# The spectral filter's channel product in two halves of 64 stationary columns

## The chip, the cores and the metric

The kernel runs on one core of a Trainium2 chip. A core has a matrix engine (TensorE, PE in the profile; its weight loads are listed apart as PEld), three engines for elementwise work (VectorE, DVE; ScalarE, ACT; GpSimd, POOL) and SyncE (SP), which here issues the DMAs. The metric is the device time of one launch in microseconds (us); the median of several runs counts.

## The reference

Four layers over an image batch of 4 x 64 x 64 x 96 (4096 tokens, 96 channels an image): a selective-scan block, a separable convolution, linear attention with a quantized feed-forward part, and a spectral filter with another such part. Only one step of the spectral filter is concerned:

```python
h = jnp.einsum('bnc,hc->bnh', x, w1)                      # 96 -> 192 channels
h = jax.nn.relu(_bn(h, ...))
X = jnp.fft.fft(h, axis=1, norm='ortho')                  # over the 4096 tokens
xr = jax.nn.relu(X.real * rd - X.imag * idg + rb)
xi = jax.nn.relu(X.imag * rd + X.real * idg + ib)
y = jnp.fft.ifft(xr + 1j * xi, axis=1, norm='ortho').real
o = jnp.einsum('bnh,ch->bnc', y, w2)                      # 192 -> 96 channels
return _bn(o, ...)
```

The last product is over channels alone and the inverse transform over tokens alone, so the kernel makes the product ahead of the inverse transform: on the real and on the imaginary part of every frequency.

## The kernel before

All arithmetic of this step is in float32. The 4096-point transform is made in two stages of 64 points each. For each image `filter_in` makes the first channel product (p_h), the gate, and the first stage (p_dft, L1337), and stores the result in DRAM (`z_s`). `filter_mid` is the stage that the change touches. It takes the 64 values of one index four at a time (`k0` = 0, 4, ..., 60: 16 groups an image). For one group it loads a piece `zl` of `z_s` (384 KB, L1362) and a piece `tw` of the table of the second stage (256 KB, L1366), each with three buffers and issued two groups ahead. Then TensorE makes

- p_dft2a (L1394): 8 products, stationary 128 x 64, moving 128 x 128, whose outputs go in turn to partitions 0 to 63 and 64 to 127 of a bank of PSUM. After the eviction `ya` holds 128 channels of four indices, with 64 frequencies of real and 64 of imaginary part side by side.
- p_dft2b (L1403): 4 products of the same kind, for the other 64 channels of the four indices, evicted into `yb`.
- p_o (L1377 and L1378): the channel product of the group before. For each of four indices `j` two products are summed in PSUM: `ya[:, j, :]` (128 channels x 128 frequencies) is stationary and the weights `w2a` (128 x 96) move; then `yb` with `w2b`, whose other half of rows is zero. The result has 128 frequency rows and 96 channels, and its eviction `os<-p_o` (L877 or L881) goes into `os_`.

After the 16 groups `filter_turn` (p_idft, L1443) and `filter_out` (p_idft, L1482) make the inverse transform.

TensorE takes a float32 product as two passes, each with a weight load and a matmul in the trace: the 64 x 4 products of L1377 stand there as 512.

Where the stage runs differs by image. Images 0 to 2 do it beside the scans of later image halves. The scans are the main work: for chunks of 128 x 1024 VectorE runs two scans and an addition (L1908, L1959, L1969), GpSimd two multiplications (L1645, L1649), ScalarE the decay `pa` (L1662) that each scan needs, and TensorE sums over states in `reduce` (py, L1676), into groups of 32 PSUM partitions. The order on each engine there is the program's: `pieces` is called after every scan step and lets the generators of the side work go on as far as their credit by engine reaches; a `yield (2.4, 0, 0, 0)` in `filter_mid` asks for 2.4 units of TensorE before a group of p_o. In that part all evictions of the stage are ScalarE's (`evacuate`), in the same queue as the decays. Image 3 is done in the tail, with no scans left; there evictions go to ScalarE and VectorE in turn, and eight banks of PSUM serve the stage in place of three.

`reduce` has an order that is of use below: where a chunk was kept apart (`dl`), it adds two terms into the same 32 partitions and then goes to the next 32:

```python
for j in (2 * c + k for c in chunks for k in range(2)):
    terms = [Ss[n, q]] + ([dls[n, 0]] if q == 0 and n in apart else [])
    for i, x in enumerate(terms):
        nc.tensor.matmul(py[32 * j : 32 * j + 32, :], lhsT=red, rhs=x[...], ...)
```

Of the kernel before, what the change touches and what calls it, by code (L numbers as in the profile page):

```python
# [30 lines left out]
N1 = 64  # L31
# [42 lines left out]
def layers(ctx: ExitStack, tc: tile.TileContext, a: dict, out):  # L74
# [4 lines left out]
    nc = tc.nc  # L79
# [43 lines left out]
    def steps_past(since, n):  # L123

        while ordered[0] and clock[0] < since + n:
            yield NEXT
# [746 lines left out]
    def evacuate(dst, src, relu=False):  # L873

        flip[0] ^= 1
        if ordered[0] or flip[0]:
            nc.scalar.activation(dst, src, AF.Relu if relu else AF.Copy)  # L877
        elif relu:
            nc.vector.tensor_scalar(dst, src, 0.0, None, ALU.max)
        else:  # L880
            nc.vector.tensor_copy(dst, src)  # L881
# [13 lines left out]
    def rest(b, take, deep, x1t=None, held=None):  # L895
# [461 lines left out]
        def filter_mid(wk, os_):  # L1357


            def load(k0):  # L1360
                z = wk.tile([128, 3, 4, N1], F32, tag="zl", name="zl", bufs=3)
                nc.sync.dma_start(  # L1362
                    z.rearrange("p h k c -> p h (k c)"), z_s[b][:, :, k0 * N1 : (k0 + 4) * N1]
                )
                tw = wk.tile([128, 4, 128], F32, tag="tw", name="tw", bufs=3)
                nc.sync.dma_start(tw, a["dft2"][:, k0 : k0 + 4, :])  # L1366
                return z, tw, clock[0]

            nxt = [load(0), load(4)]
            yield (0, 0, 0, 0, 5)  # L1370
            yield NEXT
            yield NEXT
            before = None

            def project(k0, ya, yb, po):
                for j in range(4):
                    nc.tensor.matmul(po[:, j, :], lhsT=ya[:, j, :], rhs=w2a, start=True, stop=False)  # L1377
                    nc.tensor.matmul(  # L1378
                        po[:, j, :], lhsT=yb[:, j // 2, :], rhs=w2b[:, j % 2, :],
                        start=False, stop=True,  # L1380
                    )

            for k0 in range(0, N1 + 4, 4):
                if k0 < N1:
                    pa, give_a = yield from take("p_dft2a", 128)
                    pa = pa.rearrange("p (k m) -> p k m", m=128)
                    z, tw, since = nxt.pop(0)
                    yield from steps_past(since, LANDING)
                    yield (2.4, 0, 0, 0, 2.6)
                    if k0 + 8 < N1:  # L1390
                        nxt.append(load(k0 + 8))
                    for j in range(4):
                        for hc in range(2):
                            nc.tensor.matmul(  # L1394
                                pa[hc * N1 : (hc + 1) * N1, j, :], lhsT=z[:, hc, j, :],
                                rhs=tw[:, j, :], start=True, stop=True,
                            )
                    pb, give_b = yield from take("p_dft2b", 128, 256)
                    pb = pb.rearrange("p (k m) -> p k m", m=128)
                    yield (0.8, 0.6, 0, 0)  # L1400
                    for j in range(4):
                        at = N1 * (j % 2)
                        nc.tensor.matmul(  # L1403
                            pb[at : at + N1, j // 2, :], lhsT=z[:, 2, j, :], rhs=tw[:, j, :],
                            start=True, stop=True,
                        )
                    ya = wk.tile([128, 4, 128], F32, tag="ya", name="ya", bufs=2 * deep)
                    evacuate(ya, pa, relu=True)
                    give_a()
                if before is not None:  # L1410
                    po, give = yield from take("p_o", 128, 4 * C)
                    po = po.rearrange("p (k c) -> p k c", c=C)
                    yield (2.4, 0, 0, 0)
                    project(*before, po)
                if k0 < N1:
                    yield (0, 0.4, 0, 0)
                    yb = wk.tile([128, 2, 128], F32, tag="yb", name="yb", bufs=2 * deep)
                    evacuate(yb, pb, relu=True)
                    give_b()
                if before is not None:  # L1420
                    yield (0, 0.5, 0, 0)
                    evacuate(
                        os_[:, :, before[0] : before[0] + 4], po.rearrange("p k c -> p c k")
                    )
                    give()
                before = (k0, ya, yb)
# [384 lines left out]
    aside, weights, head, start = Region(tc), Region(tc), Region(tc), Region(tc)  # L1811
# [300 lines left out]
```

## Time and profile before

| | |
|---|---|
| median of 3 runs | 5775.93 us (5759.04 to 5779.57) |
| the profiled execution, its own time | 5793.85 us |
| its span, first to last instruction | 5792.0 us |
| busy, share of the span: TensorE, VectorE, ScalarE, GpSimd | 72%, 84%, 52%, 76% |
| TensorE's mean granted clock | 0.764 of full |
| p_o: passes recorded (L1377 and L1378) | 512 and 512, median 275 ns each |
| p_dft2a: passes recorded | 1024, median 273 ns |
| ScalarE's waits for p_o (`os<-p_o`) | 79.5 us, 42 times |

A line of the timeline or of the chain has the start in microseconds from the start of the span, the duration, engine, line, operation, and the tiles written and read; "x2" after it is the number of instructions merged in it, and the bracket at the end is how long the engine stood idle before it and what released it. The time of a matmul in the trace holds its way through the array: passes that follow each other overlap, so the distance between their starts is what one costs.

### The profile page before, as it was taken

The numbers are of one execution on the slowest core, as the hardware profiler recorded it, in microseconds if no ns is written. First come the engines' busy times: TensorE is split into PE (matmuls) and PEld (weight loads), VectorE is DVE, ScalarE is ACT, GpSimd is POOL, SyncE is SP. The second block draws the span as 40 slices with busy tenths as digits, with TensorE's granted clock in tenths as the row PEclk, the third lists the DMA queues.
The fourth block names the chain that finished last, engine by engine and source line by source line (L and its number), as shares of the span: only waits on it lengthen the run. The fifth ranks groups of instructions, "written<-read, shape, count | busy, mean of one in ns | idle before, by whom it ended". The sixth has DMA issues, their size and how long they took to land. (4 is left out here: it accounts for less than half of the span.)

```text
span 5792.0 us, 65076 instructions
## 1 busy us (share of the span) xinstructions
PE 4191.9 (72%) x19770; PEld 1625.2 (28%) x19770; DVE 4882.4 (84%) x3649; ACT 3015.3 (52%) x4184; POOL 4418.5 (76%) x2164
## 2 busy tenths in 40 slices
PE   8878887879855776664576776666777667667778
PEld 4422222222211221241331221334222124323346
DVE  4188988888899898998799999999999999878564
ACT  4767766766663356545444446435544544434233
POOL 1488887888898788888778989888898898867200
PEclk9889897888866876666677876668778666877788
DMA  4388868876799878788988868679987678986013
GB/s 123 113 216 227 237 195 240 230 212 189 203 255 234 225 206 227 208 236 244 250 232 229 220 184 221 197 216 249 233 229 202 169 207 235 254 224 177 23 42 102
DMA packets 470107, 1174.80 MB, mean 203 GB/s; under 512 B 90768, under 2 KB 155900, under 8 KB 469628
## 3 DMA queue, kind: packets, MB, share of 16 engines
q1 hardware_dynamic: 469756, 1170.64, 74.1%
q8 instruction: 157, 2.57, 0.2%
q14 instruction: 194, 1.59, 0.1%
HBM read 1013.53 MB, written 156.76 MB: 202 GB/s over the span
## 5 line engine op out<-in xcount | busy, mean ns | idle before, releaser
L1649 POOL TENSOR_TENSOR S<-S,rep 128x1024 f32<-128x1024 f32 x768 | 1807.6, 2356 | 560.7 <-DVE S L1969 518.2
L1662 ACT ACTIVATE pa<-dl,nega 128x1024 f32<-128x1024 f32 x1152 | 1285.0, 1117 | 1446.7 <-DVE S L1969 1086.7
L1645 POOL TENSOR_TENSOR B<-B,rep 128x1024 f32<-128x1024 f32 x768 | 1798.6, 2357 | 114.3 <-DMA B<-du_s 54.2
L1908 DVE TENSOR_TENSOR_SCAN S<-pa,S,B 128x1024 f32<-128x1024 f32 x576 | 1352.8, 2349 | 316.1 <-ACT pa L1662 130.1
L1676 PE MATMUL py<-S,red 128*32 128x512 f32 x3072 | 916.3, 853 | 753.0 <-POOL S L1649 509.6
L1959 DVE TENSOR_TENSOR_SCAN pa<-pa,edge,B 128x1024 f32<-128x1024 f32 x438 | 1029.7, 2351 | 50.7 <-ACT pa L1662 50.7
L1969 DVE TENSOR_TENSOR S<-S,pa 128x1024 f32<-128x1024 f32 x630 | 763.6, 1212 | 1.9
L1908 DVE TENSOR_TENSOR_SCAN S<-pa,B 128x1024 f32<-128x1024 f32 x192 | 436.6, 2274 | 50.2 <-ACT pa L1662 36.3
L1676 PEld LDWEIGHTS py<-S,red 128*32 128x32 f32 x3072 | 110.4, 126 | 1238.0 <-POOL S L1649 708.9
L1959 DVE TENSOR_TENSOR_SCAN pa<-pa,B 128x1024 f32<-128x1024 f32 x192 | 441.0, 2297 | 5.3
L402 PE MATMUL p_conv<-low,conv_w 128*96 128x512 f32 x864 | 437.6, 658 | 10.1 <-ACT u L414 7.6
L154 ACT COPY side<-side 96x256 f32<-96x256 f32 (+1 forms) x448 | 279.2, 630 | 176.2 <-DMA deltaT_s<-side 74.9
L1959 DVE TENSOR_TENSOR_SCAN dl<-pa,edge,B 128x1024 f32<-128x1024 f32 x138 | 323.1, 2341 | 21.0 <-ACT pa L1662 9.3
L1250 POOL CAST h<-y 128x1536 fp8e5<-128x1536 f16 x64 | 95.5, 1492 | 305.2 <-ACT y L886 284.1
L1654 POOL TENSOR_TENSOR dl<-dl,rep 128x1024 f32<-128x1024 f32 x138 | 325.7, 2360 | 0.1
L402 PE MATMUL p_conv<-high,conv_w 64*96 64x512 f32 (+1 forms) x576 | 266.3, 599 | 0.0
L1072 PE MATMUL p_mean<-t,centre 96*96 96x512 f32 x256 | 176.4, 801 | 100.8 <-ACT sq L1064 48.1
L1676 PE MATMUL py<-dl,red 128*32 128x512 f32 x552 | 227.9, 742 | 24.2 <-POOL dl L1654 24.2
L402 PEld LDWEIGHTS p_conv<-low,conv_w 128*96 128x96 f32 x864 | 149.4, 181 | 315.6 <-issue 289.2
L1684 ACT COPY ys<-py 128x512 f32<-128x512 f32 x384 | 221.9, 578 | 20.0 <-PE py L1676 16.3
L647 PE MATMUL p_y<-side,ident 96*96 96x512 f32 x336 | 208.2, 767 | 33.4 <-DVE q L1115 11.0
L953 PE MATMUL p_l<-x,taps 96*96 96x504 f32 (+3 forms) x432 | 206.2, 630 | 16.0 <-DMA x<-x 12.1
(262 smaller groups left out, 6035.1 us busy)
## 6 DMA issues: line engine op xcount, KB each, us to landing
dl<-delta_s SPq DMA_DIRECT2D x768, 256.0 KB
B<-du_s SPq DMA_DIRECT2D x768, 256.0 KB
B<-duT_s SPq DMA_DIRECT2D x768, 256.0 KB
dl<-deltaT_s SPq DMA_DIRECT2D x768, 256.0 KB
z_s<-z SPq DMA_DIRECT2D x48, 512.0 KB
zl<-z_s SPq DMA_DIRECT2D x64, 384.0 KB
side<-y_s SPq DMA_DIRECT2D x120, 192.0 KB
rep<-bc_s SPq DMA_DIRECT2D x64, 256.0 KB
```

Source lines behind the costliest of these rows:

```text
L154: nc.scalar.copy(o.rearrange("p (w h) -> p w h", h=HW), t[:n, :].rearrange("p (h w) -> p w h", w=HW)[:, q * w : (q + 1) * w, :],)
L402: nc.tensor.matmul(p, lhsT=conv_w[: src.shape[0], k, oc * C : (oc + 1) * C], rhs=src[:, ky : ky + RPB, kx : kx + HW], start=(k == 0), stop ...
L647: nc.tensor.matmul(p, lhsT=ident[:C, :C], rhs=x, start=(j == 0), stop=(j == 2))
L1645: nc.gpsimd.tensor_tensor(Bs[n, q], Bs[n, q], reps[n // NG, 0, q], ALU.mult)
L1649: nc.gpsimd.tensor_tensor(Ss[n, q], Ss[n, q], reps[n // NG, 1, q], ALU.mult)
L1654: nc.gpsimd.tensor_tensor(dls[n, 0], dls[n, 0], reps[n // NG, 1, 0], ALU.mult)
L1662: nc.scalar.activation(pa, dls[n, q], AF.Exp, scale=nega[:, g : g + 1])
L1676: nc.tensor.matmul(py[32 * j : 32 * j + 32, :], lhsT=red, rhs=x[:, k * BLK : (k + 1) * BLK], start=(i == 0), stop=(i == len(terms) - 1),)
L1684: nc.scalar.copy(ys, pys.pop((n, half)))
L1908: nc.vector.tensor_tensor_scan(s, pas[q], Bs[n, q], Ss[n, q - 1][:, CH - 1 : CH] if q else 0.0, ALU.mult, ALU.add,)
L1959: nc.vector.tensor_tensor_scan(to[:, ::-1], pas[q][:, ::-1], Bs[n, q][:, ::-1], edge if k else 0.0, ALU.mult, ALU.add,)
L1969: nc.vector.tensor_tensor(Ss[n, q], Ss[n, q], to, ALU.add)
```

## The change

For each index `j` the two products of p_o are made twice, with 64 of the 128 stationary columns each: first frequencies 0 to 63 into partitions 0 to 63 (`ya` part, then `yb` part), then 64 to 127 into partitions 64 to 127. What is computed is the same, and so are the tiles, their buffers and the evictions.

```diff
             def project(k0, ya, yb, po):
                 for j in range(4):
-                    nc.tensor.matmul(po[:, j, :], lhsT=ya[:, j, :], rhs=w2a, start=True, stop=False)
-                    nc.tensor.matmul(
-                        po[:, j, :], lhsT=yb[:, j // 2, :], rhs=w2b[:, j % 2, :],
-                        start=False, stop=True,
-                    )
+
+                    for at in (slice(0, N1), slice(N1, 128)):
+                        nc.tensor.matmul(
+                            po[at, j, :], lhsT=ya[:, j, at], rhs=w2a, start=True, stop=False
+                        )
+                        nc.tensor.matmul(
+                            po[at, j, :], lhsT=yb[:, j // 2, at], rhs=w2b[:, j % 2, :],
+                            start=False, stop=True,
+                        )
```

`N1` is 64.

## The prediction

> **What bounds the kernel now.** I read the slices first, then the chain that ended last, then timelines of the places where p_o stands.
>
> ```profile
> PE   8878887879855776664576776666777667667778
> DVE  4188988888899898998799999999999999878564
> ...
> PE 2%; DVE 0%; ACT 0%; DMA 0%; SPq 0%; issue 0%; POOL 0%; POOLq 0%; ACTq 0%
> PE p_dft2a L1394 0%; PE p_o L1377 0%; PE p_o L1378 0%; PE p_idft L1443 0%; PE p_idft L1482 0%; PE p_rstd L1124 0%; PE p_mean L1072 0%; PE p_dft2b L1403 0%; PE p_dft L1337 0%; PE p_f L1241 0%; PE p_f L1261 0%; DMA tw<-in_dft 0%; SPq L1349 0%; PE p_var L1054 0%; DVE y L881 0%
> ```
>
> The chain goes back only through the tail, and there it is nearly all TensorE, p_o second in it. The product p_o runs 64 times: 16 groups (k0) for each of four images, each of 8 products, and a float32 product is two recorded passes, hence the x512 on each of its two lines. Images 0 to 2 do it inside the scans (near 2690 to 2897, 3905 to 4007, 5006 to 5226 us), where VectorE is the full engine. Image 3 does it in the tail, from 5656.95 us, where nothing is left to hide TensorE. One tail step in the chain, and in the timeline:
>
> ```profile
> 5672.64 1.02 PE p_dft2a L1394 x16
> 5673.66 0.44 PE p_dft2b L1403 x8
> 5676.06 1.02 PE p_dft2a L1394 x16
> ```
> ```profile
> 5672.57 1.09 PE L1394 MATMUL p_dft2a<-tw,zl 128*64 128x128 f32 x16
> 5673.49 0.61 PE L1403 MATMUL p_dft2b<-tw,zl 128*64 128x128 f32 x8
> 5674.03 0.46 PE L1377 MATMUL p_o<-w2a,ya 128*128 128x96 f32 x2
> ...
> 5674.33 0.39 PE L1378 MATMUL p_o<-w2b,yb 128*128 128x96 f32 x2
> 5674.55 0.39 PE L1377 MATMUL p_o<-w2a,ya 128*128 128x96 f32 x2
> ```
>
> To be seen: the step is 3.42 us (5672.64 to 5676.06), all TensorE. Two p_o passes start every 0.22 us, 0.112 us each. The 64-column passes of p_dft2a come faster although they stream more columns: 16 in 0.87 us, two every 0.109, because two sit in the two halves of the array at once (single records start 7 ns apart). Between the last p_dft2b stream and the first p_o stream, and again on the way out, lie about 0.2 us in which nothing streams.
>
> In the scans p_o matters through ScalarE, which works in order:
>
> ```profile
> 3957.38 0.63 PE L1378 MATMUL p_o<-w2b,yb 128*128 128x96 f32 x2
> 3958.05 0.49 ACT L877 ACTIVATE os<-p_o 128x384 f32<-128x384 f32 x1 [3.06 <-PE p_o L1378]
> 3958.44 1.11 ACT L1662 ACTIVATE pa<-dl,nega 128x1024 f32<-128x1024 f32 x1
> 3959.64 2.35 DVE L1908 TENSOR_TENSOR_SCAN S<-pa,S,B 128x1024 f32<-128x1024 f32 x1 [1.66 <-ACT pa L1662]
> ```
>
> ScalarE stood 3.06 us before the eviction of p_o, the decay pa is queued behind it, and the scan on VectorE lost 1.66 us waiting for pa. So some bursts are on the path in the scans too.
>
> **What the Trainium skill says.** "TensorEngine Tiling (Array Packing)", Key Properties: tiles of the array run weight loads and matmuls independently, and a change of tiling mode drains the array. The trace agrees: the pairs 7 ns apart, and the 0.2 us on each side of p_o (no such gap between p_dft2a and p_dft2b). "TensorE: Matmul & The Clock Gate", LDWEIGHTS, has the load take time by stationary columns (128 / 1.2 = 107 ns): the trace agrees, since 96 moving columns come at 0.112 us with 128 stationary, and 64 moving with 96 stationary at 0.087 (p_idft L1482, 11.08 us for 128), so p_o is held by its load, not by its stream. The same page, Part 3, "What overlaps and what doesn't", calls matmuls strict FIFO with monotone starts. That would decide this case: the new order is two products in one half, then two in the other. The trace differs from it. reduce (L1676) has exactly that order where a chunk was kept apart: S, dl into columns 0 to 31, then S, dl into the next 32:
>
> ```profile
> 2866.54 0.15 PEld L1676 LDWEIGHTS py<-S,red 128*32 128x32 f32 x4
> 2866.54 1.06 PE L1676 MATMUL py<-S,red 128*32 128x512 f32 x4
> 2866.91 2.30 DVE L1959 TENSOR_TENSOR_SCAN pa<-pa,B 128x1024 f32<-128x1024 f32 x1
> 2866.99 0.12 PEld L1676 LDWEIGHTS py<-dl,red 128*32 128x32 f32 x2 [0.31 <-issue]
> 2867.42 1.03 PE L1676 MATMUL py<-dl,red 128*32 128x512 f32 x4
> ```
>
> All four S passes lie ahead of all four dl passes; the second S started 13 ns after the first (single records), past the dl in front of it. Eight passes took 1.85 us until 2868.39, where one after another they need 8 x 0.43 = 3.4 (their spacing within one group). I let the measurement decide: each column group has its own queue.
>
> **The change part by part.** It removes 8 products per group and adds 16 of half the width: 16 more passes and 16 more loads, 512 more products in the program. Order and waits of ScalarE, VectorE, GpSimd and SP stay as they are, and no DMA moves; no wait is added; the eviction still waits for the last product. The planner's cost (2.4 a group) is unchanged.
>
> *Price of a pair of new passes.* 96 columns against p_dft2a's 128: 0.109 x 96/128 = 0.082 us. From below: p_idft L1443 (64 stationary, 64 moving) takes 11.46 us for 192 pairs, 0.060, its load. From above: no overlap, 2 x 0.082 = 0.164. I take 0.082, because the reduce pattern overlapped fully.
>
> *Tail.* Step: p_dft2a 8 x 0.109 = 0.87, p_dft2b 4 x 0.109 = 0.44, p_o 16 x 0.082 = 1.31, and no change of mode: 2.62. Saved 3.42 - 2.62 = 0.80. From 5656.95 to 5704.77 there are 14 steps: 11.2 us. The last two groups follow each other (3.54 us to the last record's end): 32 pairs are 2.6, saved 0.9. Together 12. What is late next: the evictions take VectorE 1.25 us at most in a step (ya 0.69, os 0.56). The loads (zl 384 KB, tw 256 KB) moved at 197 GB/s with a DMA share of 0.61 (5670 to 5684 us); at 2.62 us they need 0.61 x 3.42/2.62 = 0.80, and 5640 to 5651 held 262 GB/s. The load issued at 5674.14 had landed at 5678.7, 4.5 later; it is used three steps on, after 7.9 - 1.6 = 6.3. Spare 1.8 us. If that cover fails, the tail gains only part: zero at worst.
>
> *Scans.* A burst, first to last record, is 1.75 us at full clock and 3.31 at half. New: 0.05 + 15 x 0.082 = 1.29, and at half clock 2.54. Saved 0.46 or 0.77. For each of 48 bursts I took the smallest of this saving, ScalarE's idle time before os, and VectorE's idle time before the scan whose pa stood right behind os: 16 bursts count, 8.6 us in all (3.0, 2.8 and 2.8 by image). The other 32 cost nothing and give nothing: the eviction was late for other reasons or pa waited for VectorE. DMA is busy 0.88 to 0.94 there, so a little may be taken back at a landing: I take 8. From both sides: 0 and 20 (all 34 bursts before which ScalarE stood idle, some 0.6 us each).
>
> Sum: 12 + 8 = 20. Against the profiled execution's own 5793.85: 5774. That run lay 18 above the median; against 5775.93 the forecast is 5756.
>
> **Rivals.**
> - *Tail only.* In the scans DMA and GpSimd (93.9 of 110 us busy from 3900 to 4010) take the gain back. For: the DMA shares. Against: VectorE waited 8.3 us for pa there and hardly for anything else. 5776 - 12 = 5764.
> - *More than counted.* Earlier bursts also free banks and let the next p_dft2a start, ScalarE waiting 11.1 us for these in that window. 5776 - 12 - 20 = 5744.
> - *Slower: the halves run one after another.* If the second half starts only when the first half's two products are through, all 32 passes take 0.082 each, 2.63 a group. Tail step 0.87 + 0.44 + 2.63 = 3.94, +0.52 in 16 groups, +8; scans 2.63 - 1.75 = +0.9 in the same 16 bursts, +14. 5798. It decides from where a pair takes over 0.13 us (3.42 - 1.31 = 2.11 for 16). Against it stands the reduce record; for it, that this is one pattern with 32 columns and long streams.
> - *The change doesn't do what it says:* the pairs overlap partly, near 0.13, and gain and loss cancel: 5776.
>
> **How the numbers follow.** Forecast 0.60, tail only 0.18, more 0.10, slower 0.08, nothing 0.04. The bound of 0.5% is 29 us, about what a measurement of this kernel tells from no change (its own three runs differ by 20). The likeliest, 5756, has 5742 to 5768 with that spread. The range 5738 to 5779 takes in tail only, nothing and most of the larger gain, and leaves out the serial rival and a gain over 38. Faster by over 0.5% (below 5747): 0.10 of the forecast's lower end and 0.08 of the larger gain, 0.18. Slower by over 0.5% (above 5805): half of the serial rival, 0.04. Within: 0.78.
>
> **What would show it.** In the tail, p_dft2a should start every 2.6 us in place of 3.42 and the new p_o passes two every 0.082 us; a burst in the scans 1.3 us. No gap between p_dft2b and p_o. ScalarE's waits for p_o should fall from 79.5 us by some 20. Wrong, if p_dft2a waits for tw in the tail, if pairs take over 0.13 us, or if VectorE's idle time in the three stretches doesn't move with the bursts.

## The result, and the profile after

| | before | after |
|---|---|---|
| median of 12 runs each | 5776.65 us | 5762.98 us |
| range of the runs | 5757.87 to 5787.43 | 5748.22 to 5782.66 |
| profiled execution's span | 5792.0 us | 5769.7 us |
| tail: first to last p_o record | 51.4 us | 39.4 us |
| ScalarE's waits for p_o, whole program | 79.5 us | 54.7 us |

The ratio is 0.9977, with a 95% interval of 0.9966 to 0.9988: 13 us faster, 7 to 20 with the interval. That is a real gain, but one under the 0.5% that the prediction set as its bound. Of the 20 us forecast, the 12 of the tail came and the 8 of the scans did not.

The chain of the page after the change (the lines of p_o are L1379 and L1382 in the new kernel, and those behind them move on by four):

```profile
PE p_dft2a L1398 0%; PE p_idft L1447 0%; PE p_idft L1486 0%; PE p_o L1379 0%; PE p_o L1382 0%; PE p_rstd L1124 0%; PE p_dft L1337 0%; PE p_dft2b L1407 0%; PE p_mean L1072 0%; PE p_f L1241 0%; PE p_f L1261 0%; DMA tw<-in_dft 0%; SPq L1349 0%; PE p_var L1054 0%; DVE y L881 0%
```

The products of the inverse transform (p_idft), which stood behind p_o in this list, now stand ahead of it. The steps of the tail in the chain (start, duration, what):

```profile
5649.30 0.87 PE p_dft2a L1398 x16
5650.17 0.44 PE p_dft2b L1407 x8
5651.93 0.87 PE p_dft2a L1398 x16
```

and in the timeline:

```profile
5650.39 0.39 PE L1379 MATMUL p_o<-w2a,ya 128*64 128x96 f32 x4
...
5650.55 0.39 PE L1382 MATMUL p_o<-w2b,yb 128*64 128x96 f32 x4
...
5650.72 0.39 PE L1379 MATMUL p_o<-w2a,ya 128*64 128x96 f32 x4
```

A step is 2.63 us where it was 3.42. Four passes start every 0.165 us (5650.39, 5650.55, 5650.72), so a pair takes 0.0825. No idle time stands in a bracket between p_dft2b, p_o and the next p_dft2a.

The place in a scan that the prediction showed has this counterpart (ScalarE and VectorE in the timeline):

```profile
3959.75 0.49 ACT L877 ACTIVATE os<-p_o 128x384 f32<-128x384 f32 x1 [2.71 <-PE p_o L1382]
3960.14 1.11 ACT L1666 ACTIVATE pa<-dl,nega 128x1024 f32<-128x1024 f32 x1
3961.34 2.35 DVE L1912 TENSOR_TENSOR_SCAN S<-pa,S,B 128x1024 f32<-128x1024 f32 x1 [1.65 <-ACT pa L1666]
```

The scan lost 1.65 us here, as before (1.66), although this burst took 1.78 us from first to last record and not 3.31. It had begun later. Ahead of it on TensorE stood a p_dft2a that had waited 4.67 us for its piece of the table (and behind that `reduce`, which waited 0.33 us for GpSimd):

```profile
3953.06 1.98 PE L1398 MATMUL p_dft2a<-tw,zl 128*64 128x128 f32 x16 [4.67 <-DMA tw<-in_dft]
```

The view of waits has the sum for TensorE in this stage, that of image 1 (engine and line, released by, total us, times, longest). Before, from 3897.1 to 4021.9 us:

```profile
PE p_dft2a L1394 <- DMA tw<-in_dft: 1.7, 1, 1.7
```

After, in the same stage:

```profile
PE p_dft2a L1398 <- DMA tw<-in_dft: 20.6, 9, 4.7
...
ACT os L877 <- PE p_o L1382: 15.2, 7, 4.2
```

TensorE's busy time in this stage fell by 8.7 us, and its waits for the table `tw`, the stage's own load, rose by 18.9. VectorE, which has to become less idle if the stage is to get shorter, stood idle 10.3 us of it before and 9.6 after. That the loads took the gain is so far a guess from these sums; the experiments test it.

### The profile page after: what moved, and what is told of

It is laid out like the page before. It is cut to its first block, busy times and chain, and to the rows that moved or that the text cites. A ratio compares the mean times of both kernels' runs of the same rounds, so it can differ in the third digit from the quotient of the medians.

```text
span 5769.7 us, 67124 instructions
## 1 busy us (share of the span) xinstructions
PE 4143.8 (72%) x20794; PEld 1595.1 (28%) x20794; DVE 4882.8 (85%) x3649; ACT 3017.0 (52%) x4184; POOL 4421.9 (77%) x2164
## 5 line engine op out<-in xcount | busy, mean ns | idle before, releaser
L1688 ACT COPY ys<-py 128x512 f32<-128x512 f32 x384 | 222.1, 578 | 19.4 <-PE py L1680 18.9
```

The source lines that it names most:

```text
L1688: nc.scalar.copy(ys, pys.pop((n, half)))
```

## The experiments

The stage of an image is measured below between the same two scans of VectorE in every kernel: from some 10 us before its first burst of p_o to some 15 after the last.

**1. The tail alone.** The halves are used only where no scans run (`ordered[0]` is false), that is, for image 3.

```diff
+                halves = (slice(0, N1), slice(N1, 128)) if not ordered[0] else (slice(0, 128),)
                 for j in range(4):
-                    for at in (slice(0, N1), slice(N1, 128)):
+                    for at in halves:
```

> Halves for image 3 alone; images 0 to 2 as before. My theory (TensorE is the path in the tail, so its whole saving shows): tail step 2.63 us in place of 3.42, first to last p_o record of the tail 39.4 us in place of 51.4, total 12 us below the kernel before; the scans as before. Rival, all of the gain from the tail: the total falls by the whole 13 to 14 us. Rival, the tail's gain is taken back by what follows (table loads, the inverse transform): under 6 us.

Ratio to before 0.9978 (0.9966 to 0.9989), 12.7 us faster, as much as the whole change. First to last p_o record of the tail 39.4 us.

**2. The scans alone.** The same edit with the condition reversed.

> Halves for images 0 to 2, full width for image 3. My theory (the eviction of p_o stands before the decay on ScalarE, so VectorE waits less): bursts 1.3 us, ScalarE's waits for p_o in the scans down by some 20 us, total 4 to 8 us below the kernel before. Rival, tail only: the waits fall too, but the total is within 2 us of before. The tail step stays at 3.42 us in both.

Ratio 1.0000 (0.9990 to 1.0009): within 6 us of before, and none found. ScalarE's waits for p_o fell from 79.5 to 58.9 us all the same. In the stage of image 1 p_dft2a waited 14.5 us for `tw` (6.1 us in experiment 1, where the scans have full width), and VectorE stood idle 11.9 us. My theory of the scans falls here. What took the gain was still open: the loads, or a stall that is made good elsewhere whatever the loads do.

**3. and 4. The scans with fewer loads, at full width and in halves.** In the scans the groups after the third use the first three pieces of `zl` and `tw` again, so part of the output is not the reference's.

```diff
+            kept_loads = []
             def load(k0):
+                if ordered[0] and k0 >= 12:
+                    return *kept_loads[k0 // 4 % 3], clock[0]
...
                 nc.sync.dma_start(tw, a["dft2"][:, k0 : k0 + 4, :])
+                kept_loads.append((z, tw))
```

> The kernel before, but in the scans only the first three groups of an image load zl and tw; later groups use those tiles again (their values, and so part of the output, are not the reference's). This takes some 8 MB of DMA out of each of the three stages. Theory (the loads set the pace of these stages, so a shorter p_o buys nothing there): the stages get shorter, the stage of image 1 from 124.8 us to some 118, the total falls by 5 to 25 us. Rival (VectorE, ScalarE and TensorE pace them, the loads only fit in): the total stays within 3 us of before.

> The changed kernel with the same loads left out. Theory: with DMA out of the way the shorter bursts count, so it lies below few_loads_full by the tail's 12 us and some 5 to 8 us more, 17 to 20 in all; the stage of image 1 is 2 to 3 us shorter than in few_loads_full. Rival (the stall behind p_o is made good elsewhere in any case): 12 us below few_loads_full, the stages alike within 1 us.

Both were run a second time:

> few_loads_full once more (in the scans the loads of zl and tw of all groups after the third are left out, so the values are not the reference's), to see how much of the stage times is chance. Theory (a stage takes the longer of its loads and its chain of p_o, ScalarE and VectorE): stages of images 0, 1 and 2 within 3 us of the first time (204.2, 124.9, 208.9 us), total some 50 us below the kernel before.

> few_loads_halves once more. Theory: the stage of image 1 again some 4 us shorter than with full-width p_o (121.0 against 124.9 the first time), the total 15 to 20 us below few_loads_full_again: the tail's 12 and a few from the scans. Rival: image 1 within 1 us of the full-width one, total 12 us below.

| stage, us | image 0 | image 1 | image 2 | ratio to before |
|---|---|---|---|---|
| full width (before; 1) | 229.0; 226.9 | 124.8; 124.8 | 241.2; 234.3 | |
| halves (after; 2) | 228.5; 229.8 | 124.1; 126.5 | 234.5; 237.3 | |
| fewer loads, full width | 204.2; 203.5 | 124.9; 124.9 | 208.9; 207.3 | 0.9902 (0.9879 to 0.9924); 0.9925 (0.9911 to 0.9939) |
| fewer loads, halves | 201.7; 201.4 | 121.0; 121.1 | 212.3; 206.7 | 0.9863 (0.9842 to 0.9884); 0.9891 (0.9871 to 0.9912) |

The view by stretches for the stage of image 1 (stretch, length, busy us and count of PE, PEld, DVE, ACT and POOL, TensorE's clock, share of the DMA engines, GB/s): before,

```profile
3897.10:4021.90 124.80, 91.66 (x916) 66.69 (x916) 114.50 (x74) 60.57 (x91) 107.36 (x47) 0.85 0.92 252
```

the scans alone in halves,

```profile
3879.30:4005.80 126.50, 84.58 (x1172) 60.85 (x1172) 114.59 (x75) 60.40 (x91) 107.32 (x47) 0.84 0.92 251
```

fewer loads at full width,

```profile
3887.30:4012.20 124.90, 91.68 (x916) 66.33 (x916) 114.47 (x75) 60.50 (x91) 107.34 (x47) 0.84 0.70 189
```

and fewer loads in halves:

```profile
3860.10:3981.00 120.90, 81.99 (x1172) 59.05 (x1172) 114.43 (x74) 60.19 (x91) 107.46 (x47) 0.85 0.70 192
```

To be seen: taking TensorE's work down alone (91.7 to 84.6 us busy) leaves the stage where it was, and taking the DMA share down alone (0.92 to 0.70) does too. (With all loads the stage took 123.0 and 124.6 us in experiments 6 and 9, which have halves in the scans as well, so single runs with halves lie from 123.0 to 126.5, around the 124.8 of full width.) Only both together shorten it, by 3.9 us both times. Image 1's stage is held by two things of nearly equal length. GpSimd's own work isn't one of them: its busy time stays at 107 us while the stage gets shorter.

That the 3.9 us came by the way that the prediction took, VectorE's waits for the decay, is in the waits of this stage with fewer loads, at full width and in halves:

```profile
DVE S L1913 <- ACT pa L1667: 8.3, 9, 1.7
```
```profile
DVE S L1917 <- ACT pa L1671: 4.0, 8, 0.8
```

(8.4 and 2.4 us the second time.) VectorE's idle time fell by 3.9 us, from 10.4 to 6.5: all that the stage got shorter.

Images 0 and 2 are held by loads: leaving them out gives some 24 and 30 us at full width. In image 2 it is the scans' own loads, `B` and `dl`, that are waited for, before and after the change alike:

```profile
POOL B L1645 <- DMA B<-du_s: 42.7, 12, 8.7
```
```profile
POOL B L1649 <- DMA B<-du_s: 43.5, 11, 8.4
```

ScalarE waited another 40.5 and 38.8 us for `dl` there. With fewer loads at full width the two waits were 0.4 and 1.9 us, with fewer loads in halves 12.6 and 18.2 (5.2 and 8.3 the second time): the loads that are left are waited for again. The halves then give 2.3 us in image 0, and nothing clear in image 2 (+3.4 and -0.6). My estimate for fewer loads, 5 to 25 us in total, was low: it was 57 and 43. That image 1 would get shorter by the loads alone was wrong. The halves lie 22.6 and 19.6 us below full width with fewer loads (from the ratios, each with an uncertainty of some 14 to 18), in keeping with the tail's 12 and a few from the scans; by the totals alone this isn't settled, by the stage of image 1 it is.

**5. The halves one after the other.** All eight products of columns 0 to 63, then all eight of 64 to 127.

```diff
-                for j in range(4):
-                    for at in (slice(0, N1), slice(N1, 128)):
+                for at in (slice(0, N1), slice(N1, 128)):
+                    for j in range(4):
```

> The same 16 products of a group, first all eight of columns 0 to 63, then all eight of 64 to 127. If each column group has a queue of its own, filled far enough ahead (8 products), the halves still overlap: tail step 2.63 us. If the look-ahead is shorter than 8 products, or products are taken strictly in order, they run one after another: 32 passes of 0.082, step 3.9 us, slower than before.

Neither value: the step was 3.41 us (p_dft2a of the tail at 5653.75 and 5657.16). Its one run took 5786.86 us, within the range of the kernel before. The timeline of its tail:

```profile
5658.69 0.33 PE L1378 MATMUL p_o<-w2a,ya 128*64 128x96 f32 x2
5658.86 0.33 PE L1381 MATMUL p_o<-w2b,yb 128*64 128x96 f32 x2
5659.02 0.39 PE L1378 MATMUL p_o<-w2a,ya 128*64 128x96 f32 x4
5659.19 0.39 PE L1381 MATMUL p_o<-w2b,yb 128*64 128x96 f32 x4
5659.41 0.33 PE L1378 MATMUL p_o<-w2a,ya 128*64 128x96 f32 x2
```

Two passes in 0.165 us are one half alone, four are both at once. Both run together only for 4 passes of each (two products), at the seam of the two halves; another such seam lies on each side, with p_dft2b and the next p_dft2a. So TensorE goes past products that wait for one half, but only two of them. The changed kernel's runs of two fit; runs of three or four were not tried.

**6. Products alternating between the halves.** For each index: `ya` low, `ya` high, `yb` low, `yb` high.

```diff
+                halves = (slice(0, N1), slice(N1, 128))
                 for j in range(4):
-                    for at in (slice(0, N1), slice(N1, 128)):
+                    for at in halves:
                         nc.tensor.matmul(
                             po[at, j, :], lhsT=ya[:, j, at], rhs=w2a, start=True, stop=False
                         )
+                    for at in halves:
                         nc.tensor.matmul(
```

> The halves alternate after every product (ya low, ya high, yb low, yb high). Halves one after another in runs of eight left only the last 4 passes of each half beside the other half, so TensorE looks two products past a waiting one, and runs of two as in the changed kernel just fit: this order can gain nothing, tail step 2.63 us. If runs of two cost part of the overlap, the step is shorter, down to 2.5.

The step was 2.63 us; its one run took 5755.17 us. As expected, this order gains nothing more in the tail.

**7. Both widths mixed.** The `ya` product at 128 columns, the `yb` product in halves, for each index in turn.

```diff
-                        nc.tensor.matmul(
-                            po[at, j, :], lhsT=ya[:, j, at], rhs=w2a, start=True, stop=False
-                        )
+                    nc.tensor.matmul(po[:, j, :], lhsT=ya[:, j, :], rhs=w2a, start=True, stop=False)
```

> The ya product at full width, the yb product in halves, alternating for each index: 8 changes of column width in a group in place of 2. My theory: a change costs 0.16 us (the kernel before: 3.42 - 0.87 - 0.44 - 16 x 0.112 = 0.32 for two), so the tail step is 0.87 + 0.44 + 8 x 0.112 + 8 x 0.082 + 8 x 0.16 = 4.1 us. Rival, a change costs nothing by itself and only the load counts: 2.9 us.

The chain of its tail:

```profile
5654.51 0.87 PE p_dft2a L1395 x16
...
5656.53 0.39 PE p_o L1377 x2
5656.92 0.32 PE p_o L1379 x4
5657.24 0.39 PE p_o L1377 x2
...
5658.65 0.87 PE p_dft2a L1395 x16
```

The step is 4.14 us; 4.1 was expected with 0.16 us for a change of width. An index takes 0.71 us (5656.53 to 5657.24) where its passes alone need 2 x 0.112 + 2 x 0.082 = 0.39. In the scans the same kernel shows the other side of this balance: its longer bursts (2.65 us at full clock) made the stage of image 1 134.9 us, 10 more than before, and left images 0 and 2 at 228.8 and 237.8. Its one run took 5804.74 us.

**8. Quarters.** Four products of 32 columns in place of two of 64.

```diff
-                    for at in (slice(0, N1), slice(N1, 128)):
+                    for at in (slice(32 * k, 32 * k + 32) for k in range(4)):
```

> Four products of 32 stationary columns for each of ya and yb. If the stream is what holds the halves (0.082 us for 96 columns), four groups at once still need 4 passes of 0.082 for an index, and two changes of column width come back at 0.16 each: tail step 0.87 + 0.44 + 1.32 + 0.32 = 2.95 us. If the load still held them, quarters would be faster than halves: step below 2.6.

The chain of its tail:

```profile
5656.25 1.02 PE p_dft2a L1397 x16
5657.71 0.32 PE p_o L1378 x8
5658.03 0.17 PE p_o L1381 x8
...
5659.24 1.02 PE p_dft2a L1397 x16
```

The step is 2.99 us. Eight passes, four groups at once, take 0.17 us as four did in halves: the stream of 96 columns holds it, not the load. Quarters cost 0.36 us more a step than halves, and two changes of width on both sides of p_o, as forecast, make 0.32 of it. Its one run took 5782.2 us.

This trace also says more on experiment 5. The first pass of each quarter starts within 0.04 us (single records, 5660.63 to 5660.67 us), the fourth with nine passes ahead of it in the program that have not started, three of each other quarter. So the bound of two products is not one for TensorE as a whole; counted for each column group, it fits both traces.

**9. The same on the last product of the transform.** On top of the change, p_idft of `filter_out` (96 stationary, 64 moving columns) in three products of 32.

```diff
-                    nc.tensor.matmul(
-                        p[:, j, :], lhsT=vs[:, n0 + j, :], rhs=table[:, n0 + j, :],
-                        start=True, stop=True,
-                    )
+                    for at in (slice(32 * k, 32 * k + 32) for k in range(3)):
+                        nc.tensor.matmul(
+                            p[at, j, :], lhsT=vs[:, n0 + j, at], rhs=table[:, n0 + j, :],
+                            start=True, stop=True,
+                        )
```

> The changed kernel, with the last product of the inverse transform (96 stationary columns, 64 moving, 0.087 us a pass, 11.1 us in the tail) made in three products of 32 columns. It is held by its load as p_o was, so the same theory says: three groups at once, one triple of passes in 0.055 to 0.060 us, 128 of them in 7 to 7.7 us in place of 11.1, total 3 to 4 us below the changed kernel, 16 to 18 below the kernel before. Rival, what comes after (VectorE's evictions, the table's loads) holds it: under 1 us below the changed kernel.

Ratio to before 0.9979 (0.9968 to 0.9989), as against 0.9977 for the changed kernel. With such intervals the totals alone can't tell a gain of 3 to 4 us from none; the trace can. The groups of its stretch from 5719 to 5735 us (busy us, mean ns, then idle us before it and the releaser):

```profile
L1473 DVE SCALAR_TENSOR_TENSOR t<-p_idft,s,t 96x512 f32<-96x512 f32 x8 | 10.2, 1334 | 2.7 <-PE p_idft L1487 2.7
L1487 PE MATMUL p_idft<-os,vs 128*32 128x64 f32 x384 | 8.8, 220 | 2.8 <-issue 2.8
```

The passes did run as the theory has it: three at once, a triple every 0.056 us. But TensorE waited three times in between, so they spread over 11.4 us as against 10.8 at full width, and nothing was gained. The rival fits: the eight evictions of this stage take VectorE 10.2 us. What TensorE waited for each time the trace doesn't name, so that it was these evictions and not the table's loads isn't shown.

## Why the prediction was right, and where it was not

The time lay in the range, 7 us above the value given. That alone says little for the sum: the range also held no change at all, and 5763 us is the value of the rival *tail only*, 5764. The tail was forecast by its mechanism; that the total came out so near although the term of the scans failed is owed to that term's small size and to a wide range, and so in part to luck.

- *Price of a pair, 0.082 us.* Measured 0.0825. That each column group goes on by itself was right, and the reduce record was the right evidence for it, against the strict order that the Trainium skill states in "TensorE: Matmul & The Clock Gate", Part 3. Experiments 5 and 8 bound it: two products ahead within a column group, with runs of eight no more.
- *The load is what held p_o at full width.* Right: a pass took 0.112 us with 128 stationary columns, and 0.0825 with 64 and with 32, so there the stream holds it (experiment 8). The serial rival and partial overlap fall with this.
- *No change of width any more.* Right: 0.16 us for each, an estimate from the step of the kernel before that experiment 7 reproduced with eight of them; two make 0.32 of the 0.79 us saved in a step. "TensorEngine Tiling (Array Packing)", Key Properties, names the drain; experiments 7 and 8 put a price on the change, and no run here shows what happens inside the array during it.
- *Tail 12 us.* Right: 51.36 to 39.44 us between first and last p_o record, 11.9, and 12.7 by the ratio of experiment 1. The DMA cover held: from 5655 to 5669 us the share was 0.78 at 257 GB/s (forecast 0.80), and p_dft2a waited for no load from 5645 to 5686.
- *Scans 8 us.* Wrong: 0, in experiment 2 between -6 and +5 us by its interval. The bursts shortened as computed (1.29 to 1.36 us, and 2.52 at half clock, forecast 1.29 and 2.54), and ScalarE's waits for p_o fell by 25 us, 20 of them in the scans (experiment 2). The step that failed is the count of "the smallest of this saving, ScalarE's idle time before os, and VectorE's idle time". It added up single waits as if nothing else set the pace, and then took off only "a little" for a DMA share of 0.88 to 0.94. What the runs showed in its place: the stages took the longer of their loads and their chain of engines. In images 0 and 2 the loads are the longer by some 24 and 30 us; the waits of image 2 for its loads (42.7 and 40.5 us) stood in the trace of the kernel before, and the count passed them over. In image 1 both are about 124. A wait removed from the chain of image 1 comes back as a wait for `tw` (1.7 us before, 20.6 after). The prediction's own sign of being wrong came true, too: VectorE's idle time in the stage of image 1 didn't move with the bursts (10.3 us before, 9.6 after, 11.9 in experiment 2). The rival *tail only* was the case, with DMA as its reason. GpSimd, the rival's other reason, didn't hold image 1; for images 0 and 2 it wasn't tested apart from the loads it waits for.
- *Size of the chain's gain.* With fewer loads the forecast 3.0 and 2.8 us for images 0 and 1 became 2.3 and 3.9, in image 1 by VectorE's shorter waits for the decay. The mechanism by ScalarE's queue was thus not wrong, it was covered. For image 2 no gain could be told from chance; there the waits for loads came back.

## What to carry to other kernels

A product whose stationary operand is wider than its stream, held by its weight load, gains from being cut into column groups that run side by side, unless something else holds the time, as in experiment 9. It gains most where its neighbours have the same group width (0.79 us a step with halves, 0.43 with quarters) and where runs within one group are short: two float32 products did, eight did not. Before summing stalls in a stage with a high DMA share (0.88 to 0.92 in these), measure it once with fewer loads: if the loads are as long as the chain of engines or longer, a stall removed comes back as a wait for a load. A stage at balance shows no gain from either side alone, but loses at once when one side gets longer (10 us in image 1 with mixed widths, in one run).

## What was not expected of the hardware

In these runs TensorE's look-ahead past products that wait for their column group ended after two float32 products of that group, that is 4 passes with their loads: with runs of eight, 4 of 16 passes overlapped at each seam (experiment 5). The groups count apart: with quarters, nine passes of three other groups were gone past at once (experiment 8).

Neither the rate nor the share of the DMA engines' time told by itself whether loads held a stage. In the tail 257 GB/s took a share of 0.78, and p_dft2a waited for no load; in the stage of image 1, 252 GB/s took 0.92, and a shorter p_o gained nothing there. The stage of image 2 had a share of 0.88 before, when GpSimd waited 42.7 us for `B`, and again 0.88 with fewer loads at full width, when it waited 0.4.
